# Tiles 2 and 3 turned by VectorE instead of TensorE, tiles 26 and 27 given their bias in the bank, and a new order, in a fused mean, linear and ReLU kernel

## The chip, the cores and the metric

The kernel runs on one core of one Trainium2 chip. The metric is the device time of one execution in microseconds (us), median of the runs. "us" also stands for the times in the trace, which are counted from the first instruction of the program.

## The reference

`x` has the shape (4, 1024, 512), `cond` (4, 256), `W` (1536, 512) and `b` (512), all float32. What is computed:

```python
hidden = concatenate([cond_512, cond_512], axis=-1)
x_mean = mean(x, axis=1, keepdims=True)
fused = concatenate([x, x_mean * ones_L, hidden[:, None, :] * ones_L], axis=-1)
relation = relu(einsum('bld,do->blo', fused, W) + b)
return x + relation
```

So every row of `x` is multiplied by the first third of `W`; the mean of its batch row by the second third and the condition by the last third are the same for all 1024 rows of a batch row, and together with `b` they make one bias vector per batch row. ReLU, and `x` is added.

## The kernel before

The 4096 rows of `x` are 32 tiles of 128 rows; batch row r is tiles 8r to 8r+7. A tile's product is 128x512 by 512x512. The contraction has J = 4 blocks of 128. Since float32 is split into a high and a low part (float32r), each block takes three matmuls, high by high, low by high and high by low (`product`, L355, L365): 12 for each tile, 384 in all, each 512 columns wide except that tile 31 is done in two halves of 256 columns. All of them add up in one of five PSUM banks (`bank`, L352, tile number modulo 5).

TensorE wants `x` with the contraction on the partitions, so every tile must be turned. Tiles 0 to 3, units 0 to 3 of one tile each, are turned by TensorE (`BY_PE`, L76): `x` arrives in its natural layout (tasks `X0.0` to `X0.3`), is gathered by a copy (`y`, L231), and a matmul by the identity turns it (`T`, L262, four for each tile). The other 28 tiles are seven units of four tiles, numbered 4 to 10. For them `x` is loaded a second time, in four quarters of 32 partitions (`Z`, L176, rows of 512 B), into one of three z buffers, and VectorE turns a block of all four tiles at once (`T`, L264, 32 by 32 blocks). After that ScalarE copies the turned block into the high part and takes its row sums for the mean in the same instruction (`h`, L270), and VectorE or GpSimd subtracts for the low part (`l`, L276). The high and low parts of `W` are made likewise (`wh`, L213, `wl`, L221).

The bias of a batch row is summed up on VectorE from the loaded parts of `W` (`c`, L302, `m`, L318), folded and spread over the partitions by one matmul by ones (`pb`, L342), and copied out by ScalarE (`bc`, L346).

A finished bank leaves in one of three ways (`WAYS`, L19). K (tiles 0 to 11): copied out (`K`, L428), bias added by GpSimd (`b`, L435), ReLU on ScalarE (`r`, L443), `x` added by GpSimd or VectorE (`F`, L450). B (tiles 12 to 27): `K`, L439, adds the bias on the way out, then `r` and `F` as before. I (tiles 28 to 31): ScalarE writes the bias into the bank before its first product (`P`, L418, L398), and one VectorE instruction does ReLU and the sum (`F`, L422, L402). Then SyncE stores the tile (`S`).

The order in which each engine does all this is the list `ORDER` (L22): a name is a task, `@d`, `@a` and `@p` put it on VectorE, ScalarE or GpSimd, and `fill` is a matmul on zeros. Nothing else schedules the work. `p2.0.1` is tile 2, block 0, second of the three matmuls; `p3.0` is all three; `31.0l` is a half. All loads but one and all stores are issued by SyncE in the order of the list, and share one queue.

```python
UNITS = [(t, 1) for t in range(4)] + [(t, 4) for t in range(4, NT, 4)]
BY_PE = (0, 1, 2, 3)
X_PARTS = {0: [(i, 1) for i in range(4)]}
```

## Time and profile before

| what | us |
|---|---|
| median of 3 runs | 101.08 |
| the three runs | 100.9, 101.08, 105.57 |
| the profiled execution | 101.22 |
| its span in the trace | 99.5 |
| outside of the span | 1.72 |

The profile is of one execution. The span runs from the first instruction of the program to the last one; the execution has 1.72 us around it. PE is TensorE's matmul queue, PEld its loads of the stationary operand, DVE is VectorE, ACT ScalarE, POOL GpSimd, SP SyncE, which only issues transfers here. A matmul's duration in the trace overlaps the next one's: what it costs is the distance from start to start.

### The profile page before, as it was taken

The page shows a single profiled execution, that of the slowest core. Times are in us where ns is not written, and L with a number is a line of the kernel's source. Part 1 is how long each engine was busy: PE and PEld are TensorE (multiplying, and loading weights), DVE is VectorE, ACT ScalarE, POOL GpSimd, SP SyncE. Part 2 cuts the span into 40 slices and gives each one's busy share as a digit, 9 for nine tenths or more (in the row PEclk, how much of TensorE's full clock was granted, in tenths as well). Part 3 has the DMA queues.
Part 4 walks back from the last instruction along what each step waited for, and adds up shares of the span by engine and source line. Part 5 has one row for each costly group of instructions (what it writes and reads, how often), then busy time and mean ns, then how long its engine had stood idle before and what let it go on. Part 6 is the DMA issues. An engine that isn't in the chain of part 4 may idle for free.

```text
span 99.5 us, 1446 instructions
## 1 busy us (share of the span) xinstructions
PE 95.0 (96%) x425; PEld 76.2 (77%) x425; DVE 80.2 (81%) x144; ACT 58.2 (58%) x153; POOL 65.1 (65%) x65
## 2 busy tenths in 40 slices
...
GB/s 43 376 375 239 210 199 212 278 394 314 222 209 212 215 254 269 209 223 275 259 212 242 328 294 268 308 133 264 390 315 366 208 275 285 404 406 406 398 385 123
DMA packets 25361, 27.36 MB, mean 275 GB/s; under 512 B 1413, under 2 KB 16009, under 8 KB 25354
## 3 DMA queue, kind: packets, MB, share of 16 engines
q1 hardware_dynamic: 25210, 27.01, 100.8%
q10 hardware_dynamic: 144, 0.26, 0.7%
q8 instruction: 3, 0.05, 0.2%
...
## 4 chain that ended last, share of the span: by engine, by line
PE 93%; ACT 2%; DVE 1%; issue 0%
PE po L365 87%; PE po L132 4%; ACT hi L271 1%; PE acc L343 1%; DVE x L403 1%; ACT o L235 1%; PE po L262 0%; DVE lo L277 0%; PE acc L262 0%; PE px L262 0%; DVE warm L123 0%; DVE one L124 0%
## 5 line engine op out<-in xcount | busy, mean ns | idle before, releaser
L365 PE MATMUL po<-w_hi,lo 128*128 128x512 f32 (+1 forms) x132 | 50.6, 386 | 0.1
L365 PE MATMUL po<-w_lo,hi 128*128 128x512 f32 (+1 forms) x132 | 50.5, 385 | 0.0
L365 PE MATMUL po<-w_hi,hi 128*128 128x512 f32 (+1 forms) x132 | 50.4, 386 | 0.0
L277 POOL TENSOR_TENSOR lo<-xT,hi 128x512 fp32r<-128x512 f32 x14 | 18.6, 1335 | 23.5 <-ACT hi L271 23.5
L365 PEld LDWEIGHTS po<-w_hi,lo 128*128 128x128 f32 x132 | 24.9, 188 | 5.7 <-DVE lo L277 0.7
L365 PEld LDWEIGHTS po<-w_hi,hi 128*128 128x128 f32 x132 | 24.7, 188 | 5.3 <-issue 0.4
L365 PEld LDWEIGHTS po<-w_lo,hi 128*128 128x128 f32 x132 | 24.8, 188 | 4.7
L454 POOL TENSOR_TENSOR x<-o,x 128x512 f32<-128x512 f32 x19 | 26.3, 1406 | 1.5 <-ACT o L447 1.5
L447 ACT ACTIVATE o<-o 128x512 f32<-128x512 f32 x28 | 16.2, 620 | 1.6 <-DVE o L440 1.3
L436 POOL TENSOR_TENSOR o<-o,bias 128x512 f32<-128x512 f32 x12 | 15.5, 1309 | 1.4 <-ACT bias L347 1.4
L271 ACT ACTIVATE hi<-px 128x512 fp32r<-128x512 f32 (+1 forms) x20 | 9.9, 495 | 4.9 <-DVE px L264 2.6
L319 DVE SCALAR_TENSOR_TENSOR acc<-w_mean,tot,acc 128x512 f32<-128x512 f32 x16 | 12.0, 750 | 0.6
L440 DVE TENSOR_TENSOR o<-po,bias 128x512 f32<-128x512 f32 x16 | 10.7, 677 | 1.7 <-PE po L365 1.7
L277 DVE TENSOR_TENSOR lo<-px,hi 128x512 fp32r<-128x512 f32 (+1 forms) x20 | 10.9, 558 | 1.1 <-ACT hi L271 1.0
L271 ACT ACTIVATE hi<-xT 128x512 fp32r<-128x512 f32 x14 | 8.8, 627 | 3.0 <-DVE xT L264 3.0
L264 DVE STREAM_TRANSPOSE px<-z 128x512 f32<-128x512 f32 x14 | 9.9, 707 | 0.0
L264 DVE STREAM_TRANSPOSE xT<-z 128x512 f32<-128x512 f32 x14 | 9.6, 690 | 0.2
L432 ACT ACTIVATE o<-po 128x512 f32<-128x512 f32 x10 | 5.6, 599 | 5.6 <-PE po L365 5.6
L454 DVE TENSOR_TENSOR x<-o,x 128x512 f32<-128x512 f32 x9 | 8.0, 914 | 0.9 <-ACT o L447 0.9
L303 DVE SCALAR_TENSOR_TENSOR acc<-wc,cT,acc 128x512 f32<-128x512 f32 x8 | 6.0, 746 | 0.3
L132 PE MATMUL po<-warm 128*128 128x512 bf16 x9 | 4.1, 614 | 1.0 <-DVE one L124 1.0
L327 ACT ACTIVATE fold<-acc 64x512 f32<-64x512 f32 x4 | 2.4, 597 | 4.4 <-DVE acc L319 4.4
...
## 6 DMA issues: line engine op xcount, KB each, us to landing
out_dram<-x SPq DMA_DIRECT2D x31, 256.0 KB, 4.0
z<-in_x_dram SPq DMA_DIRECT2D x28, 256.0 KB, 8.0
...
x<-in_x_dram SPq DMA_DIRECT2D x4, 256.0 KB, 3.9
...
w_mean<-in_L_cond_W_dram SPq DMA_DIRECT2D x4, 256.0 KB, 7.4
x<-in_L_cond_W_dram SPq DMA_DIRECT2D x3, 256.0 KB, 4.1
x<-in_L_cond_W_dram ACTq DMA_DIRECT2D x1, 256.0 KB
```

The lines of the kernel that those rows point to most:

```text
L132: nc.tensor.matmul(ps_o[2], lhsT=warm, rhs=warm.rearrange("p (o d) -> p o d", o=1).to_broadcast([P, 4, P]), start=True, stop=True,)
L264: nc.vector.transpose(xT.rearrange("p (n q e) -> p n q e", q=Q // E, e=E), zs[z_of(u)][:, : n * NQ].rearrange("p n (q j e) -> p n j q e", ...
L271: nc.scalar.activation(his[buf][:, col : col + m], xT, AF.Copy, accum_out=sums[:, r, j, s : s + 1])
L277: nc_of[e].tensor_tensor(los[buf][:, col : col + m], xT, his[buf][:, col : col + m].bitcast(F32), ALU.subtract)
L303: nc.vector.scalar_tensor_tensor(acc, wc[:, k], cT[:, k, r : r + 1], acc, ALU.mult, ALU.add)
L319: nc.vector.scalar_tensor_tensor(acc, w_mean[:, j, :], tot[:, r, j : j + 1], acc, ALU.mult, ALU.add)
L365: nc.tensor.matmul(v, lhsT=a[:, col : col + P], rhs=m, start=WAYS[t] != "I" and key not in done, stop=done.count(key) == 3 * J - 1, skip_g ...
L432: nc.scalar.activation(o, bank(t), AF.Copy)
L436: nc_of[e].tensor_tensor(o, o, biases[r], ALU.add)
L440: nc.vector.tensor_tensor(o, bank(t), biases[r], ALU.add)
L447: nc.scalar.activation(o, o, AF.Relu)
L454: nc_of[e].tensor_tensor(x_tile(t), o, x_tile(t), ALU.add)
```

## The change

- Tiles 2 and 3 become unit 2 of two tiles, `UNITS` and `BY_PE` say so. Their natural loads `X0.2` and `X0.3` leave the head of the program and become one load, `X0.2`, in its middle. Four half-size quarters `Z2.0` to `Z2.3` (8 of the 16 columns of z, 128 KB each) are issued behind the blocks of `W`. Two gathers and eight TensorE turns go; four VectorE turns of 128x256 come, and the eight `h` and eight `l` of 128x128 become four and four of 128x256. The old units 4 to 10 are now 3 to 9.
- Tiles 26 and 27 go way I instead of way B.
- `ORDER` is a new list throughout. Work changes engines in it: `wl0` and `wl1` go to GpSimd, `wh0`, `wh1` and `wh3` to ScalarE, and at the end GpSimd adds `x` to tiles 18 and 25 and no longer to tile 24.

```diff
-WAYS = "KKKKKKKKKKKKBBBBBBBBBBBBBBBBIIII"
+WAYS = "KKKKKKKKKKKKBBBBBBBBBBBBBBIIIIII"
...
-W0@a X0.0 fill X0.1 relu fill X0.2 fill W1 fill W2 fill fill W3 fill y0.2@d y0.0@d X0.3 y0.1@d fill Z4.0 wh0r@d T0.0
+W0@a X0.0 fill X0.1 relu fill W1 fill W2 fill fill W3 fill Z2.2 y0.1@p fill y0.2@d Z2.1 y0.0@d T0.1 T0.2 wh0l@a Z2.0
...
+p1.2.1 T2.0 p1.1.2 T2.1 Z4.1 p1.3.2 h2.0 p1.0.0 T2.3 p0.3.1 l2.0@d p0.3.2 h2.3 K1@d p2.0 h2.1 Z4.3 l2.3@d p3.0
+l2.1@p l0.1@d T2.2 p3.3 h2.2 Z4.2 l2.2@d p2.3 p0.2.1 p0.1.1 C p2.2 K0@d B p3.1 V T3.2 M2 p2.1 T3.1 h3.2 p3.2 M3 h3.1
+l3.2@d p4.2 K2@a T3.3 l3.1@p T3.0 p7.2 M1 h3.3 p5.1 h3.0 l3.3@p l3.0@d p6.1 M0 p4.0 to0 T4.1 Z5.2 p5.0 Z5.0 T4.0
...
-    UNITS = [(t, 1) for t in range(4)] + [(t, 4) for t in range(4, NT, 4)]
-    BY_PE = (0, 1, 2, 3)
-    Y_PARTS = {0: [(0, 1), (1, 1), (2, 2)], 1: [(0, 2), (2, 2)], 2: [(0, 2), (2, 2)]}
+    UNITS = [(0, 1), (1, 1), (2, 2)] + [(t, 4) for t in range(4, NT, 4)]
+    BY_PE = (0, 1)
+    Y_PARTS = {0: [(0, 1), (1, 1), (2, 2)], 1: [(0, 2), (2, 2)]}
     X_SLOT = [2, 3, 4, 5, 0, 1, 2, 3]
-    X_PARTS = {0: [(i, 1) for i in range(4)]}
+    X_PARTS = {0: [(0, 1), (1, 1), (2, 2)]}
...
-    sums = sb("sums", [P, B, J, 5])
+    sums = sb("sums", [P, B, J, 4])
...
-    pre = sb("pre", [P, J, 3])
+    pre = sb("pre", [P, J, 2])
...
-        2: [(pa, 1), (pb, 1), (pa, 2), (pb, 2)], 3: [(acc, 2), (acc, 3), (o4, 2), (o4, 3)],
...
-                xT = (turned if j % 2 else ps_x)[j // 2]
+                xT = (turned if j % 2 else ps_x)[j // 2][:, :m]
```

`to0`, which adds up the row sums of batch row 0, has two additions instead of three, since there are four units in it and not five.

What SyncE issues first, before: `x_65` takes tiles 0 to 3, `x_63` the blocks of `W` (block 0 goes out on ScalarE's queue), `z_69` and `z_70` the quarters of tiles 4 to 7 and 8 to 11.

```order
L146 DMA x_65<-in_x_dram 128x512 x3
L146 DMA x_63<-in_L_cond_W_dram 128x1x512 x3
L146 DMA x_65<-in_x_dram 128x512
L146 DMA z_69<-in_x_dram 32x16x128 x4
L146 DMA z_70<-in_x_dram 32x16x128 x4
L146 DMA bias_121<-in_cond_dram 4x256
```

And after, where `z_69` is first used for the half-size quarters of tiles 2 and 3, and `z_70` and `z_71` take tiles 4 to 7 and 8 to 11:

```order
L145 DMA x_65<-in_x_dram 128x512 x2
L145 DMA x_63<-in_L_cond_W_dram 128x1x512 x3
L145 DMA z_69<-in_x_dram 32x8x128 x4
L145 DMA z_70<-in_x_dram 32x16x128 x4
L145 DMA z_71<-in_x_dram 32x16x128 x4
L145 DMA bias_121<-in_cond_dram 4x256
```

Each block of `W` stands one place further to the front, and what followed the last block is now four short transfers with 512 B rows where one of 2 KB rows stood.

What VectorE does around its first turn, before: `lo_91` to `lo_93` are the low parts of tiles 1 to 3, `px_141` and `xT_123` the turned blocks of the first unit of four tiles.

```order
L277 TENSOR_TENSOR lo_91<-po_139,hi_76 128x128
L277 TENSOR_TENSOR lo_92<-px_141,hi_77 128x128
L277 TENSOR_TENSOR lo_93<-acc,hi_78 128x128 x2
L277 TENSOR_TENSOR lo_93<-po_140,hi_78 128x128 x2
L264 STREAM_TRANSPOSE px_141<-z_69 128x512
L264 STREAM_TRANSPOSE xT_123<-z_69 128x512
L277 TENSOR_TENSOR lo_94<-px_141,hi_79 128x512
```

And after, where the 128x256 rows are tiles 2 and 3, `o_106<-po_137` and `o_105<-po_136` are the tasks K1 and K0, and `px_142<-z_70` is T3.2, the first turn of tiles 4 to 7:

```order
L262 STREAM_TRANSPOSE px_141<-z_69 128x256
L262 STREAM_TRANSPOSE xT_123<-z_69 128x256
L262 STREAM_TRANSPOSE xT_124<-z_69 128x256
L275 TENSOR_TENSOR lo_92<-px_141,hi_77 128x256
L426 COPY o_106<-po_137 128x512
L275 TENSOR_TENSOR lo_93<-xT_124,hi_78 128x256
L275 TENSOR_TENSOR lo_90<-px_142,hi_75 128x128
L262 STREAM_TRANSPOSE px_142<-z_69 128x256
L275 TENSOR_TENSOR lo_93<-px_142,hi_78 128x256
L426 COPY o_105<-po_136 128x512
L262 STREAM_TRANSPOSE px_142<-z_70 128x512
L262 STREAM_TRANSPOSE xT_123<-z_70 128x512
```

Three turns now stand before the first low part of tile 2, and the copies K1 and K0 before the first turn of tiles 4 to 7.

What ScalarE does around the last bias, before: `bias_121` is batch row 3's, `po_139` the bank of tile 28.

```order
L447 ACTIVATE o_115<-o_115 128x512
L447 ACTIVATE o_116<-o_116 128x512
L347 ACTIVATE bias_121<-acc 128x512
L419 ACTIVATE po_139<-bias_121 128x512
L419 ACTIVATE po_136<-bias_121 128x512
```

And after, where `po_137` is the bank of tile 26 and `po_138` of tile 28:

```order
L443 ACTIVATE o_111<-o_111 128x512
L343 ACTIVATE bias_121<-acc 128x512
L415 ACTIVATE po_137<-bias_121 128x512
L443 ACTIVATE o_113<-o_113 128x512
L443 ACTIVATE o_112<-o_112 128x512
L443 ACTIVATE o_115<-o_115 128x512
L415 ACTIVATE po_139<-bias_121 128x512
L415 ACTIVATE po_140<-bias_121 128x512
```

The bias of tile 26 is now written right behind the copy of the bias itself, and TensorE's list has six matmuls (`p23.2`, `p24.3`) between `pb3` and the first product of tile 26.

## Rows read from the trace of the kernel before

**Rows 1.** The page: busy time of each engine, share of the span, instructions.

```profile
PE 95.0 (96%) x425; PEld 76.2 (77%) x425; DVE 80.2 (81%) x144; ACT 58.2 (58%) x153; POOL 65.1 (65%) x65
```

**Rows 2.** Chain that ended last, in order of time: start, us, engine, tile, line.

```profile
0.97 3.60 PE po L132 x8
...
63.00 19.04 PE po L365 x84
...
95.72 0.78 DVE x L403 x2
```

**Rows 3.** Timeline of TensorE, head: start, us, instruction; L365 products, L262 turns.

```profile
5.24 0.50 PE L365 MATMUL po<-w_hi,hi 128*128 128x512 f32 x1
...
14.04 0.39 PE L365 MATMUL po<-w_lo,hi 128*128 128x512 f32 x1
14.27 0.38 PE L262 MATMUL acc<-ident,o 128*128 128x128 f32 x2
14.41 0.48 PE L365 MATMUL po<-w_lo,hi 128*128 128x512 f32 x1
14.72 0.39 PE L365 MATMUL po<-w_hi,lo 128*128 128x512 f32 x1
```

**Rows 4.** SyncE's timeline: when the last block of W and Z4.2 were issued.

```profile
3.42 0.60 SPq L146 DMA_DIRECT2D x<-in_L_cond_W_dram  x1
...
6.39 0.49 SPq L146 DMA_DIRECT2D z<-in_x_dram  x1
```

**Rows 5.** The same two transfers: count, KB each, us from issue to landing.

```profile
x<-in_L_cond_W_dram SPq DMA_DIRECT2D x1, 256.0 KB, 4.2
...
z<-in_x_dram SPq DMA_DIRECT2D x1, 256.0 KB, 8.1
```

**Rows 6.** Stretches: busy of PE, PEld, DVE, ACT, POOL; clock, DMA share, GB/s.

```profile
4.00:6.00 2.00, 2.00 (x11) 1.38 (x9) 1.84 (x8) 1.07 (x6) 0.00 (x0) 1.00 0.98 366
10.00:12.00 2.00, 2.00 (x11) 1.65 (x10) 1.96 (x6) 0.94 (x4) 0.00 (x0) 1.00 1.23 210
64.00:66.00 2.00, 2.00 (x10) 1.66 (x9) 1.82 (x4) 1.59 (x6) 2.00 (x3) 1.00 0.32 88
...
94.00:96.00 2.00, 2.00 (x17) 1.80 (x15) 0.97 (x2) 0.00 (x0) 0.00 (x0) 1.00 1.03 391
```

**Rows 7.** Groups of instructions by line and shape: count, busy us, mean ns, idle before.

```profile
L454 POOL TENSOR_TENSOR x<-o,x 128x512 f32<-128x512 f32 x19 | 26.3, 1406 | 1.5 <-ACT o L447 1.5
...
L440 DVE TENSOR_TENSOR o<-po,bias 128x512 f32<-128x512 f32 x16 | 10.7, 677 | 1.7 <-PE po L365 1.7
L264 DVE STREAM_TRANSPOSE px<-z 128x512 f32<-128x512 f32 x14 | 9.9, 707 | 0.0
...
L454 DVE TENSOR_TENSOR x<-o,x 128x512 f32<-128x512 f32 x9 | 8.0, 914 | 0.9 <-ACT o L447 0.9
...
L271 ACT ACTIVATION_READ_ACCUMULATOR hi<-px 128x1 f32 x20 | 3.9, 195 | 0.0
...
L235 ACT ACTIVATE o<-x 128x256 f32<-128x256 f32 x2 | 0.8, 411 | 0.0
```

**Rows 8.** Timeline of VectorE, first unit of four: first turn to first low part.

```profile
16.48 0.71 DVE L264 STREAM_TRANSPOSE px<-z 128x512 f32<-128x512 f32 x1
...
17.95 0.69 DVE L277 TENSOR_TENSOR lo<-px,hi 128x512 fp32r<-128x512 f32 x1 [0.18 <-ACT hi L271]
```

**Rows 9.** Timeline around the last bias: the matmul pb3, bc3 and P28.

```profile
81.88 0.39 PE L343 MATMUL acc<-v_acc,ones 128*128 128x512 f32 x1
...
82.30 0.60 ACT L347 ACTIVATE bias<-acc 128x512 f32<-128x512 f32 x1 [0.38 <-PE acc L343]
...
82.93 0.60 ACT L419 ACTIVATE po<-bias 128x512 f32<-128x512 f32 x1
```

**Rows 10.** Timeline of the end: GpSimd's last additions of x, SyncE's last stores.

```profile
90.16 3.07 POOL L454 TENSOR_TENSOR x<-o,x 128x512 f32<-128x512 f32 x2 [1.54 <-ACT o L447]
...
96.17 0.83 SPq L146 DMA_DIRECT2D out_dram<-x  x2
```

More of the change, by code (lines that the diff above doesn't have):

```diff
@@ L42 @@
-r17@a p22.0 T9.3 F7@p X6.0 K18 p21.1 h9.3 X3.0 S5 c3.0 F8@p p22.3 r10@a S4 T10.2 p21.0 S2 S7 K20 l9.3@p p21.3 h10.2
-X5.0 l9.0@d r18@a p23.2 T10.1 F6@p p23.0 T10.3 p25.1 K21 b9@p h10.3 p22.2 T10.0 h10.1 p23.3 c3.1 h10.0 X6.1 p26.0
-X7.0 r15@a F18@d r9@a p25.3 to3 K19 F10@p r14@a p22.1 m3.0 r19@a p26.3 m3.1 F9@p p26.2 m3.2 p24.1 m3.3 F17@p S9
-p25.2 S6 K22 f3 S18 p24.0 F12@p S8 fa3 p25.0 vh3 F19@d p23.1 r20@a X7.1 F13@p p24.3 r22@a S10 K23 S17 p27.1 vl3
-r23@a l10.3@p p26.1 l10.0@d r11@a pb3 F23@d p27.2 bc3@a F11@p l10.2@d S23 P28 p27.0 S19 K25 p24.2 S12 F15@p K26 P30
@@ new lines @@
+p0.0.1 h1.1 p0.0.2 wh2@d Z3.2 h1.0 T1.3 p1.1.0 h0.3 l1.0@d p1.0.2 h1.2 wl2@d p0.2.0 h1.3 p1.2.0 wh3@a wl1@p Z3.1
+l1.1@d p1.2.2 l1.3@d p1.0.1 l1.2@d h0.1 p1.1.1 l0.2@d p0.2.2 p1.3.0 wl3@d p0.1.2 Z4.0 p0.3.0 l0.3@d p0.1.0 p1.3.1
+p1.2.1 T2.0 p1.1.2 T2.1 Z4.1 p1.3.2 h2.0 p1.0.0 T2.3 p0.3.1 l2.0@d p0.3.2 h2.3 K1@d p2.0 h2.1 Z4.3 l2.3@d p3.0
+l2.1@p l0.1@d T2.2 p3.3 h2.2 Z4.2 l2.2@d p2.3 p0.2.1 p0.1.1 C p2.2 K0@d B p3.1 V T3.2 M2 p2.1 T3.1 h3.2 p3.2 M3 h3.1
+l3.2@d p4.2 K2@a T3.3 l3.1@p T3.0 p7.2 M1 h3.3 p5.1 h3.0 l3.3@p l3.0@d p6.1 M0 p4.0 to0 T4.1 Z5.2 p5.0 Z5.0 T4.0
@@ new lines @@
+p7.0 h4.1 Z5.1 t3 as0 p7.1 t0 T4.2 h4.0 p7.3 T4.3 K3@a p4.1 l4.0@d h4.3 p6.3 K7@a ac0@d Z5.3 h4.2 p8.0 ac1@p t2 t1
+p6.2 c0.0 p4.3 Z6.0 l4.1@p c0.1 p5.3 K4@a m0.0 p5.2 Z6.1 l4.3@p m0.1 p8.1 K5@a m0.2 p6.0 Z6.3 m0.3 p9.1 l4.2@d Z6.2
+f0 p10.1 K6@a fa0 p8.3 Z7.2 vh0 p9.0 vl0 p10.2 T5.1 Z7.3 p11.3 T5.2 h5.1 p10.0 T5.3 Z7.1 l5.1@p pb0 p11.1 T5.0 bc0@a
+as1 p9.3 b2@p Z7.0 h5.2 c1.0 p8.2 h5.0 p9.2 c1.1 b0@p X4.1 h5.3 p11.0 X0.2 l5.2@d K8@a p10.3 l5.0@d to1 r0@a X1.0
+b3@p T6.0 K9@a X1.1 p13.1 K10@a T6.1 p12.2 h6.0 l5.3@p m1.0 p12.0 r3@a m1.1 h6.1 p15.0 b1@p m1.2 p15.2 m1.3 p13.3
@@ new lines @@
+F0@p r1@a p14.3 T6.2 f1 T6.3 p15.1 l6.1@p h6.2 fa1 Z9.0 p13.0 Z8.0 l6.0@d vh1 b5@p p12.1 Z8.1 h6.3 T7.0 Z9.2 p15.3
+vl1 l6.3@p p11.2 l6.2@d p13.2 T7.2 K11@a r2@a pb1 T7.1 p12.3 Z8.3 bc1@a F2@p p16.1 as2 K13 h7.2 p16.3 Z8.2 T7.3 F3@p
+h7.1 p14.2 K15 h7.3 p18.1 c2.0 Z9.1 b7@p h7.0 p18.2 c2.1 p18.0 Z9.3 l7.2@d to2 r7@a l7.1@p p16.0 K12 m2.0 p14.1 F1@p
+p14.0 m2.1 p17.1 m2.2 b4@p S1 p16.2 X2.1 m2.3 S3 p17.2 K14 b6@p X3.0 f2 p18.3 X4.0 r5@a fa2 p17.0 l7.3@p l7.0@d vh2
+p19.3 r4@a T8.2 p20.2 b10@p vl2 h8.2 p19.0 T8.1 F5@p l8.2@d p19.1 T9.2 pb2 p20.0 bc2@a T8.3 F4@p as3 p20.3 K18 r12@a
@@ new lines @@
+p17.3 K16 F7@p S4 h8.1 S0 p19.2 T8.0 r6@a X5.0 K17 p20.1 l8.1@p X2.0 h8.3 S7 p21.2 h8.0 K20 S5 l8.3@p r15@a p21.1
+l8.0@d X6.0 h9.2 S2 p22.0 T9.1 X3.1 F6@p T9.0 p25.2 h9.1 T9.3 p25.1 h9.0 b8@p S6 K19 h9.3 p25.3 X5.1 c3.0 p22.1 to3
+r8@a c3.1 b11@p p23.3 X7.0 m3.0 p21.0 b9@p m3.1 r11@a p21.3 r18@a m3.2 p25.0 X6.1 F11@p r9@a p24.1 m3.3 r10@a p24.2
+f3 F8@p p23.0 r13@a fa3 p22.2 vh3 F10@p p22.3 r19@a vl3 p24.0 K21 F9@p S10 S8 p23.1 F19@d pb3 S9 p23.2 bc3@a l9.1@p
+S11 l9.2@d P26 p24.3 K23 r21@a p26.3 r20@a F21@d p26.1 r23@a F12@p K24 S21 p26.2 P28 K22 P29 p26.0 l9.3@p S12 P27
```

36 lines of the change are left out of this document (9 added, 27 removed).

## The prediction

> **What bounds the kernel now.** I read the busy times first: TensorE is busy for 95.0 of 99.5 us, VectorE for 80, the others for less [rows 1]. Then the chain of waits in order of time: it runs on TensorE almost without a break until 95.72, then through two VectorE instructions of tile 31, then the last stores [rows 2]. 84 products take 19.04 us there, 0.2267 us each; this step is the unit of what follows. The 384 products, 372 of 512 columns and 24 halves, can't be had for less, so there are only three places where a change can gain or lose: the head, before products come at that pace; matmuls between the products; the end, behind the last one.
>
> The head is measured by one number: the start of the n-th product less (n-1) steps of 0.2267, the time by which the products run late. In the list 32 products stand before the one that starts at 14.72 [rows 3], so before it is 14.72 - 32 x 0.2267 = 7.47 us. The first product starts at 5.24 [rows 3]; of the 2.23 us between, the turns are the larger part: from 14.04 to 14.72 there are two products, 0.45 us, and two turns, so a turn costs 0.115 us, and the twelve behind the first product 1.4. The other 0.8 us are waits for copies, high and low parts.
>
> **The change part by part.** *Eight turns go.* 8 x 0.115 = 0.92 us less on TensorE, all on the path.
>
> *But TensorE has less to do early.* Only 22 of the 24 products of tiles 0 and 1 stand before `p2.0`, the first of the new unit. From 5.24 they take 22 x 0.2267 = 5.0 us, four turns 0.5 and waits as before 0.8: done at 11.5. Moving `wl0`, `wl1` and one gather to GpSimd and `wh` to ScalarE is inside this: dearer there or not, it costs nothing while tile 2 is ready later than 11.5.
>
> *When do the quarters land?* The last block of `W` was issued at 3.42 and landed 4.2 us later, at 7.6; `Z4.2`, behind `X0.3` and three quarters, was issued at 6.39 and landed at 14.5 [rows 4, 5]. Between the two lie 6.9 us. A 256 KB block of wide rows takes 0.7 us at 366 GB/s, a quarter of 512 B rows 1.25 us at 210 GB/s [rows 6]: 0.7 + 4 x 1.25 = 5.7, and 1.2 us are left as lag of the landing behind the data. After the change `X0.2` no longer stands before `W`, so the last block lands 0.7 earlier, at 6.9; the four half quarters take 4 x 0.625 = 2.5, to 9.4. The trace shows no half quarter, so the lag is bounded: none (9.4), or twice that of the four whole ones (11.8). I take the 1.2 us, for the same number of transfers in the same queue: **10.6**. The Skill speaks against the row here: the Trainium skill, DMA: Bandwidth & Descriptors, Specifications, lets transfers run at line rate from 512 B on. By that the four would take 1.4 us and land at 9.5; 210 GB/s against 366 contradicts it [rows 6].
>
> *From there to the products.* `T2.0` waits for all four quarters, 10.65. A turn of 512 columns takes 0.71 [rows 7]; one of 256 I put at 0.41, as a 256-column copy on ScalarE [rows 7], between half of 0.71 and all of it. `h2.0` then takes 0.41 and the reading of its sums 0.195, half of it overlapped: 11.6. VectorE has `T2.1` and `T2.3` before `l2.0` and starts that at 11.75, done at 12.15. `p2.0.1`, the 24th product, goes at 12.2 and is late by 12.2 - 23 x 0.2267 = 7.0. The wait of about half a microsecond in front of it is new.
>
> *Behind it, what is late next.* VectorE's queue has K1, `l2.3`, `T2.2`, `l2.2` and K0 before `T3.2`. K0 waits for `p0.1.1`, the 36th product: start 12.2 + 12 x 0.2267 = 14.9, end 0.39 later, and K0 takes 0.68, as the other reads of a bank [rows 7]. So `T3.2` starts at 16.0; its quarters, 4 x 1.25 behind, land at 15.6 and don't decide. From the first turn of a unit of four to the end of its first low part went 17.95 + 0.69 - 16.48 = 2.16 us [rows 8], with the same two turns before it as now. `p4.2.1`, the 50th product, goes at 18.2: late by 18.2 - 49 x 0.2267 = 7.1. `T3.0` and `l3.0` after it come out for `p4.0.1` at 20.9, no later than that. So the head comes down from 7.47 to 7.1: **0.37 us gained**, of the 0.92 of the turns; the rest goes into the wait for the quarters.
>
> *The second load of tiles 2 and 3* moves 0.5 MB more, 2.5 us of the queue at the rate of quarters. It pushes later loads; what hides it is the hole at 64 to 66, where the queue ran at 88 GB/s, 32% busy [rows 6]. Without that cover it reappears as stores at the end, 0.5 MB at 391 GB/s = 1.3 us.
>
> *Tiles 26 and 27.* Each loses a bank read with bias (0.68), a ReLU and an addition (0.91 on VectorE [rows 7]) and gains a write of the bias, 0.60 on ScalarE [rows 9], and one VectorE instruction, taken as the bank read's 0.68. VectorE gains 2 x 0.91 us near the end, beside TensorE: nothing on the path. The wait that it adds: `p26.3` stands six products behind `pb3`, 0.23 + 6 x 0.2267 = 1.59 us, and now needs the copy of the bias, then `P26`. From `pb3` to the end of the first such write were 82.93 + 0.60 - 81.88 = 1.65 us [rows 9], and 0.05 for the signal: **0.1 lost**. Behind `P26` on ScalarE stand ReLUs and `P28`, which has over 2 us.
>
> *The end.* F31 and the last two stores [rows 2, 10] are what they were: 0.
>
> The sum is made against the profiled execution, 101.22 with its span of 99.5: 101.22 - 0.37 + 0.1 = 100.95. The median of the runs shown is 0.14 below it: **100.8 us**.
>
> **The rivals.** *The quarters land later (slower).* Every 0.1 us after 10.6 is 0.1 us, since `l2.0`, K0 and `T3.2` shift with it. The gain is gone at a landing of 10.9; at the bound of 11.8 it is 1.2 - 0.27 = 0.9 us slower than before, 102.0. For it: the queue is already full (share 1.23) when whole quarters go through [rows 6], and those of tiles 4 to 7 are queued right behind. Against it: a block of wide rows landed within 4.2 us although issued into a full queue [rows 5].
>
> *The quarters land early.* With no lag, or at the rate of wide rows (0.7 us for 256 KB, so 1.4 for all four), they land by 9.5, `p2.0.1` goes right behind the 22 products at 11.75, K0 ends by 15.5, `p4.2.1` goes at 17.7: late by 6.6, 0.9 us gained, 100.3; with the 0.8 us of waits gone too, 100.0 at the least. For it: 9.4 is plain bytes by rate. Against: the landing of `Z4.2`, which plain bytes put at 13.3.
>
> *The end moves to GpSimd.* It was busy throughout its middle and now adds `x` once more in all (1.41 us [rows 7]), tile 25's as its last, and the stores of 25, 30 and 31 stand behind one another on SyncE. Before, its last two additions took 1.5 us each after a wait of 1.54 and ended at 93.2 [rows 10]; one more brings 94.7 if that wait stays. The last issue was in the 0.83 us from 96.17; at 0.42 for each store the one of tile 25 may go as late as 95.3 without harm. So it is covered by 0.6 us; if GpSimd slips by 2 us through waits for ScalarE, or the 0.5 MB isn't absorbed, the time is some 101.2 + 0.3 to 1.0: 101.9.
>
> *The clock falls.* The eight fills ran 0.45 us apart [rows 2], 512 columns near the lower level of 1.2 GHz, the products at 0.2267, near 2.4; the granted clock is 1.00 in every stretch that I read [rows 6]. The Trainium skill, TensorE: Matmul & The Clock Gate, What's actually happening, has the slower level as the state after idleness. If the waits around 11.5 brought it back for some ten products, that is 10 x 0.22 = 2.2 us: 103.0. Before, TensorE had waits of that size only among the turns, with no such effect.
>
> **How the numbers follow.** The forecast, quarters at about 10.6 and little else: 0.60. Quarters late enough to lose: 0.19. Early: 0.11. End at GpSimd or the stores: 0.08. Clock: 0.02. The likeliest case has its own range of 100.4 to 101.1. To hold 8 in 10 the range takes in most of the early case and of the late one: 100.2 to 101.8. A measurement of this kernel tells about 2% from no change, 2.02 us. Faster than that would be below 99.06: even the head without any wait gives only 100.0, so 0.01. Slower, above 103.1, needs the clock or two slower cases together: 0.04. Within: 0.95.
>
> **What would show it.** Right: eight turns instead of sixteen, a first 512-column product near 5.2, VectorE idle before its first 128x256 turn until 10.5 to 10.8 with a transfer of z as releaser, TensorE waiting about 0.5 us before the 23rd or 24th product, the 50th at about 18.2, products in steps of 0.227 after that, SyncE's last issue 0.3 us earlier. Wrong: the turn starting before 10 or after 11.2; waits of TensorE after 20 us (for banks, `P26`, low parts from GpSimd); a product step of 0.43; SyncE's last stores held by GpSimd instead of TensorE.

## The result and the profile after

The changed kernel took 102.79 us (median of 22 runs, 101.59 to 103.72), the kernel before 102.75 in 22 runs between them; the ratio is 1.0103 with a 95% interval of 1.0068 to 1.0138. So the change made the kernel 1.0% slower, about 1.0 us, where 0.3 us less was forecast. That is within the 2% that the prediction called no change, but 102.79, and also 1.0103 times the 101.08 shown ahead (102.1), lie above its range of 100.2 to 101.8. Some executions of either kernel (7 of 22 and 12 of 22) are in a slower state and take some per cent longer, so the ratio here (medians 102.2 and 101.3 us) and those below compare the others alone, two of six with e7_before_load and five or more with each other run.

The profiled execution took 102.06 us with a span of 100.3 us, against 101.22 and 99.5 before. Busy times of the page of the changed kernel, to be read beside [rows 1]:

```profile
PE 94.7 (94%) x417; PEld 75.3 (75%) x417; DVE 79.2 (79%) x133; ACT 57.9 (58%) x146; POOL 68.6 (68%) x69
```

TensorE has eight instructions and 0.3 us less, as the turns went; the span is longer all the same. The chain that ended last in the changed kernel, in order of time (start, us, what), beside [rows 2]:

```profile
1.63 4.54 DMA x<-in_L_cond_W_dram
...
7.36 0.29 DVE lo L275
7.66 1.28 DVE w_lo L221
...
8.98 26.85 PE po L361 x116
...
78.22 18.17 PE po L361 x90
...
96.42 0.42 DVE x L399
```

Before, the chain ran over TensorE from its fills on, with short pieces of ScalarE and VectorE between. Now TensorE's part begins at 8.98: up to there it waits for a low part of `W` on VectorE. Behind the last product stands one addition of tile 31, where the chain before had two, and then the stores. The same place in the timeline of the changed kernel, VectorE, GpSimd and TensorE:

```profile
6.81 0.43 DVE L217 CAST w_hi<-x 128x512 fp32r<-128x512 f32 x1 [0.94 <-DMA x<-in_L_cond_W_dram]
...
6.89 1.48 POOL L221 TENSOR_TENSOR w_lo<-x,w_hi 128x512 fp32r<-128x512 f32 x1 [0.63 <-ACT w_hi L215]
...
7.57 1.36 DVE L221 TENSOR_TENSOR w_lo<-x,w_hi 128x512 fp32r<-128x512 f32 x1
...
8.98 0.50 PE L361 MATMUL po<-w_lo,hi 128*128 128x512 f32 x1 [0.58 <-DVE w_lo L221]
```

`wl2` on VectorE takes 1.36 us beside `wl1` on GpSimd; the next one on VectorE, `wl3`, takes 0.68 in the same program:

```profile
9.64 0.68 DVE L221 TENSOR_TENSOR w_lo<-x,w_hi 128x512 fp32r<-128x512 f32 x1
...
10.45 0.46 DVE L262 STREAM_TRANSPOSE px<-z 128x256 f32<-128x256 f32 x1
10.82 0.73 DVE L262 STREAM_TRANSPOSE xT<-z 128x256 f32<-128x256 f32 x2
```

The last two rows are the first turns of tile 2. No idle time stands before them: VectorE was busy until 10.45, and the quarters (issued from 3.59, 5.0 us to landing in the middle) were there at 10.4. TensorE ran 22 products up to 12.5 and went on with tile 2 without a stop.

Around tile 26, ScalarE and TensorE in the timeline of the changed kernel, which answer to [rows 9]:

```profile
77.83 0.39 PE L339 MATMUL acc<-v_acc,ones 128*128 128x512 f32 x1
...
78.26 0.60 ACT L343 ACTIVATE bias<-acc 128x512 f32<-128x512 f32 x1 [1.36 <-PE acc L339]
...
78.89 0.60 ACT L415 ACTIVATE po<-bias 128x512 f32<-128x512 f32 x1
...
79.19 0.39 PE L361 MATMUL po<-w_lo,hi 128*128 128x512 f32 x1
...
79.55 0.19 PEld L361 LDWEIGHTS po<-w_hi,hi 128*128 128x128 f32 x1 [0.39 <-ACT po L415]
79.55 0.50 PE L361 MATMUL po<-w_hi,hi 128*128 128x512 f32 x1
...
79.88 0.39 PE L361 MATMUL po<-w_hi,lo 128*128 128x512 f32 x1
```

From 79.19 to 79.88 there are two steps, 0.69 us instead of 0.45: TensorE loses 0.13 us to the wait for `P26` and another 0.11 in the step behind it.

Where the 0.8 us of the two spans went, then: the 50th product starts at 18.70 (before 18.69), so the head gave nothing in this profile; tile 26 cost 0.24, and the last product starts 0.34 later, at 96.10; the rest, 0.5 us, lies behind it, in the stores. Stretches at the end of the changed kernel (busy time of PE, PEld, DVE, ACT, POOL; clock, DMA share, GB/s):

```profile
80.00:84.00 4.00, 4.00 (x19) 3.27 (x18) 3.92 (x6) 3.33 (x8) 2.77 (x2) 1.00 0.85 322
84.00:88.00 4.00, 4.00 (x20) 3.36 (x19) 1.81 (x4) 3.51 (x7) 3.54 (x3) 1.00 0.88 287
88.00:92.00 4.00, 4.00 (x20) 3.36 (x19) 3.55 (x5) 0.39 (x1) 4.00 (x4) 1.00 1.02 390
92.00:96.00 4.00, 4.00 (x27) 3.62 (x26) 1.50 (x3) 0.00 (x0) 2.19 (x2) 1.00 1.05 403
96.00:100.00 4.00, 0.38 (x4) 0.17 (x2) 0.42 (x1) 0.00 (x0) 0.00 (x0) 1.00 0.71 260
```

And of the kernel before:

```profile
80.00:84.00 4.00, 4.00 (x19) 3.30 (x19) 3.90 (x7) 2.86 (x6) 4.00 (x4) 1.00 0.89 250
84.00:88.00 4.00, 4.00 (x20) 3.30 (x19) 3.15 (x6) 3.10 (x6) 4.00 (x3) 1.00 1.05 405
88.00:92.00 4.00, 4.00 (x21) 3.36 (x20) 4.00 (x6) 1.98 (x4) 2.46 (x3) 1.00 1.06 406
92.00:96.00 4.00, 4.00 (x28) 3.58 (x26) 2.24 (x5) 0.00 (x0) 1.23 (x1) 1.00 1.04 395
```

This is the view that the prediction should have been made from. The queue is full at 405 GB/s. At 80 us both kernels have 6.5 to 6.7 MB left to move (changed: 4 x (322 + 287 + 390 + 403 + 260) GB/s x us = 6.65 MB), and 6.6 MB at 405 GB/s take 16.3 us: the data can't be out before 96.3 us, which is about when TensorE ends. So the end is tied to the stores as much as to TensorE, and a hole in the queue after 80 us can show in the time. From 80 to 96 us the changed kernel loses 16 x 405 - 4 x (322 + 287 + 390 + 403) = 870 KB, 2.2 us of a full queue; the kernel before 660 KB, 1.6 us. The changed kernel has two holes there, in stretches of 2 us:

```profile
82.00:84.00 2.00, 2.00 (x10) 1.64 (x9) 2.00 (x5) 1.75 (x4) 0.77 (x1) 1.00 0.64 238
...
86.00:88.00 2.00, 2.00 (x11) 1.69 (x11) 0.00 (x0) 1.51 (x3) 2.00 (x2) 1.00 0.73 200
```

They go with SyncE's waits (changed kernel, 79 to 98 us: what it waited for, us in total, times, the longest):

```profile
SPq L145 <- DVE x L450: 3.0, 3, 2.2
SPq L145 <- POOL x L450: 1.5, 3, 0.8
```

SyncE issues in the order of the list. At 79.3 us it comes to `S21`, whose addition on VectorE ends at 81.61, and for 2.2 us issues nothing, though the load `X7.1`, five places behind, could go: in the run that moves it ahead of `S21` it goes out at 78.79. The first hole follows. Between 86 and 90 us it stands at single stores of GpSimd's additions in the same way, and from 88 us on the rest goes through a full queue.

### The profile page after: what moved, and what is told of

The parts are those of the page before. It is cut to its first block, busy times and chain, and to the rows that moved or that the text cites. A ratio compares the mean times of both kernels' runs of the same rounds, so it can differ in the third digit from the quotient of the medians.

```text
span 100.3 us, 1413 instructions
## 1 busy us (share of the span) xinstructions
PE 94.7 (94%) x417; PEld 75.3 (75%) x417; DVE 79.2 (79%) x133; ACT 57.9 (58%) x146; POOL 68.6 (68%) x69
## 3 DMA queue, kind: packets, MB, share of 16 engines
q1 hardware_dynamic: 26282, 27.54, 99.8%
HBM read 19.40 MB, written 8.39 MB: 277 GB/s over the span
## 4 chain that ended last, share of the span: by engine, by line
PE 87%; DMA 5%; DVE 2%; ACT 1%; SPq 1%; issue 0%
PE po L361 86%; DMA x<-in_L_cond_W_dram 5%; DVE w_lo L221 1%; PE acc L339 1%; SPq L145 1%; ACT w_hi L215 1%; ACT hi L269 1%; DVE x L399 0%; DVE lo L275 0%
## 5 line engine op out<-in xcount | busy, mean ns | idle before, releaser
L275 POOL TENSOR_TENSOR lo<-xT,hi 128x512 fp32r<-128x512 f32 (+1 forms) x15 | 20.2, 1352 | 18.4 <-ACT hi L269 18.4
L443 ACT ACTIVATE o<-o 128x512 f32<-128x512 f32 x26 | 15.4, 623 | 2.6 <-POOL o L432 2.5
L269 ACT ACTIVATE hi<-px 128x512 fp32r<-128x512 f32 (+2 forms) x18 | 9.6, 532 | 6.5 <-DVE px L262 6.2
L275 DVE TENSOR_TENSOR lo<-px,hi 128x512 fp32r<-128x512 f32 (+2 forms) x18 | 10.8, 603 | 1.5 <-ACT hi L269 1.5
L269 ACT ACTIVATE hi<-xT 128x512 fp32r<-128x512 f32 (+1 forms) x16 | 9.6, 601 | 3.7 <-DVE xT L262 3.7
L262 DVE STREAM_TRANSPOSE px<-z 128x512 f32<-128x512 f32 (+1 forms) x16 | 10.8, 673 | 0.2
L262 DVE STREAM_TRANSPOSE xT<-z 128x512 f32<-128x512 f32 (+1 forms) x16 | 10.3, 647 | 0.1
L436 DVE TENSOR_TENSOR o<-po,bias 128x512 f32<-128x512 f32 x14 | 9.1, 669 | 0.0
L419 DVE SCALAR_TENSOR_TENSOR x<-po,x 128x512 f32<-128x512 f32 x5 | 3.4, 682 | 4.5 <-PE po L361 4.5
L450 DVE TENSOR_TENSOR x<-o,x 128x512 f32<-128x512 f32 x6 | 5.9, 1001 | 0.2 <-ACT o L443 0.2
```

The costliest lines, as they stand in the source:

```text
L262: nc.vector.transpose(xT.rearrange("p (n q e) -> p n q e", q=Q // E, e=E), zs[z_of(u)][:, : n * NQ].rearrange("p n (q j e) -> p n j q e", ...
L269: nc.scalar.activation(his[buf][:, col : col + m], xT, AF.Copy, accum_out=sums[:, r, j, s : s + 1])
L275: nc_of[e].tensor_tensor(los[buf][:, col : col + m], xT, his[buf][:, col : col + m].bitcast(F32), ALU.subtract)
L419: nc.vector.scalar_tensor_tensor(x_tile(t), bank(t), 0.0, x_tile(t), ALU.max, ALU.add)
L436: nc.vector.tensor_tensor(o, bank(t), biases[r], ALU.add)
L443: nc.scalar.activation(o, o, AF.Relu)
```

## The experiments

Each run was compared in five rounds with the kernel before. The table has, worked out from one profile of each kernel, the start of the 8th, 50th and last product (the 396th, since tile 31 has 24 halves; the expectations speak of the 400th), what the queue lost from 80 to 96 us (16 us at 405 GB/s less the four stretches of 4 us, divided by 405), the MB that are left to move at 88 us, the span, and the ratio to the kernel before with its interval.

| run | 8th | 50th | last | lost | left | span | ratio (95%) |
|---|---|---|---|---|---|---|---|
| before | - | 18.69 | 95.76 | 1.6 | 3.9 | 99.5 | 1 |
| changed | 8.98 | 18.70 | 96.10 | 2.2 | 4.2 | 100.3 | 1.0103 (1.0068 to 1.0138) |
| e1_wl1_vector | 8.48 | 18.22 | 95.58 | 2.1 | 4.0 | 100.8 | 1.0030 (0.9976 to 1.0084) |
| e2_pb3_early | 9.36 | 19.11 | 96.33 | 1.8 | 4.3 | 101.3 | 1.0060 (1.0002 to 1.0119) |
| e3_adds_vector | 8.70 | 18.44 | 95.84 | 2.5 | 4.2 | 100.5 | 1.0078 (1.0023 to 1.0133) |
| e4_all | 8.70 | 18.45 | 95.69 | 2.4 | 4.0 | 101.0 | 1.0080 (1.0012 to 1.0149) |
| e5_load_early | 8.45 | 18.18 | 95.57 | 1.4 | 3.5 | 99.2 | 0.9971 (0.9939 to 1.0002) |
| e6_head_queue | 8.74 | 18.48 | 95.72 | 1.1 | 3.6 | 99.8 | 0.9957 (0.9923 to 0.9990) |
| e7_before_load | - | 18.46 | 95.53 | 2.8 | 4.4 | 101.1 | 1.0155 (1.0096 to 1.0214) |
| e8_bias_out | 8.76 | 18.49 | 95.61 | 3.7 | 4.4 | 101.8 | 1.0215 (1.0173 to 1.0256) |
| e9_one_load | 8.77 | 18.49 | 95.83 | 2.3 | 4.2 | 100.4 | 1.0070 (1.0027 to 1.0113) |
| e10_head_vector | 8.37 | 18.10 | 95.31 | 1.2 | 3.4 | 99.2 | 0.9963 (0.9924 to 1.0002) |
| e11_bias_out_apart | 8.37 | 18.11 | 95.18 | 3.1 | 4.2 | 100.7 | 1.0146 (1.0072 to 1.0219) |

Read the columns against one another: the start of the last product moves by 1.2 us over these runs and doesn't order the ratios (the earliest, 95.18, has the third worst ratio). Four runs have it within 0.1 us, at 95.5 to 95.6 (e1, e5, e7 and e8), and ratios from 0.9971 to 1.0215. The queue does order them, roughly: the four slowest lost 2.2 to 3.7 us and have 4.2 to 4.4 MB left at 88 us, the three below 1 lost 1.1 to 1.4 and have 3.4 to 3.6 left. The loss is a rough measure, since it also counts stretches in which the DMA engines were busy throughout and moved less than 405 (share 1.03 at 382 GB/s, 92 to 96 us of e11).

The 8th product has to be read with care. Before it the cast of `W2` waits for a block of `W` to land, and that landing differs from profile to profile: in the seven with the changed kernel's head (the changed one, e2, e3, e5, e8, e9 and e11) the cast starts at 6.20 to 7.01 us, the 8th product 2.2 to 2.4 us behind it, at 8.37 to 9.36.

**The low part of W back on VectorE.**

```diff
-p1.2.0 wh3@a wl1@p Z3.1 l1.1@d p1.2.2
+p1.2.0 wh3@a Z3.1 l1.1@d wl1@d p1.2.2
```

> Edit: the low part of W's second quarter goes from GpSimd back to VectorE, behind the low part of tile 1's second block; nothing else moves. Theory A (the subtraction on GpSimd slows the one on VectorE beside it): VectorE's low part of W2 takes 0.7 us instead of 1.36, the eighth product starts at 8.2 to 8.4 us instead of 8.98, the 24th (first of tile 2 that is late) near 12.0, and the 400th 0.4 to 0.7 us earlier than in the changed kernel; the time is 0.4 to 0.7 us below it, at or below the kernel before. Rival B (the W blocks land late in this traffic and set the eighth product, whoever subtracts): the low part of W2 still takes over 1.1 us or starts later, the eighth product stays within 0.2 us of 8.98, the time within 0.2 us of the changed kernel. Rival C (tile 2's turns, held by VectorE and the quarters, are late anyway): the eighth product is early, but the idle time comes back at the 24th or 50th product, and the 50th still starts within 0.15 us of the changed kernel's.

`wl2` of this run, in VectorE's timeline:

```profile
6.27 0.43 DVE L217 CAST w_hi<-x 128x512 fp32r<-128x512 f32 x1 [0.33 <-DMA x<-in_L_cond_W_dram]
...
7.75 0.68 DVE L221 TENSOR_TENSOR w_lo<-x,w_hi 128x512 fp32r<-128x512 f32 x1
```

0.68 instead of 1.36: theory A holds for the mechanism. What it was worth in time isn't shown. The 8th product starts at 8.48 and the 50th at 18.22, 0.5 us earlier than in the changed kernel's profile, with no wait at tile 2 (so rival C falls); but in e5_load_early, whose head is the changed kernel's, they start at 8.45 and 18.18, and the cast of `W2` starts there when it does here:

```profile
6.27 0.43 DVE L217 CAST w_hi<-x 128x512 fp32r<-128x512 f32 x1 [0.34 <-DMA x<-in_L_cond_W_dram]
```

So the half microsecond goes with the landing, which is rival B's cause. In the run with all three edits the cast started at 7.42 and the 8th product only 1.3 us behind it; what the edit gains depends on the landing. The ratio came down by 0.7%, with intervals that overlap.

**The bias row one block, three products, earlier.**

```diff
-S8 p23.1 F19@d pb3 S9
+S8 pb3 p23.1 F19@d S9
```

> Edit: the product that spreads the third bias row stands one product earlier on TensorE; nothing else moves. Theory A (TensorE's stop at tile 26's last product delays all behind it): the bias copy and ScalarE's write of the bias into tile 26's bank end 0.2 us earlier or more, the stop of 0.13 + 0.11 us goes, the 400th product starts 0.2 us earlier and the time is 0.2 us lower than the changed kernel's. Rival B (the queue of stores sets the end, not TensorE): the stop goes, the 400th product starts 0.2 us earlier, and the last store's issue and the time stay where they are, within 0.1 us.

The stop at `p26.3` went, but half of it, 0.12 us, came back in the step behind the moved `pb3` (0.34 us), whose operand was now ready only 0.06 us before it. The run's own head was worse by chance, and shows the hold that GpSimd has on VectorE more sharply than the edit made for it. GpSimd's `wl1`, and VectorE's cast of `W2` beside it:

```profile
6.95 1.28 POOL L221 TENSOR_TENSOR w_lo<-x,w_hi 128x512 fp32r<-128x512 f32 x1 [0.77 <-ACT w_hi L215]
...
7.01 1.50 DVE L217 CAST w_hi<-x 128x512 fp32r<-128x512 f32 x1 [1.04 <-DMA x<-in_L_cond_W_dram]
```

The cast began 0.06 us after GpSimd's subtraction, and what takes 0.43 elsewhere took 1.50. What TensorE's 0.24 us are worth in time this run can't say.

**Three additions to VectorE.**

```diff
-l9.0@d p29.2 r22@a F15@p
+l9.0@d p29.2 r22@a F15@d
...
-p27.3 F13@p
+p27.3 F13@d
...
-P31r F14@p
+P31r F14@d
```

> Edit: three of the late additions (tiles 15, 13, 14) go from GpSimd to VectorE, at their places in the order. Theory A (GpSimd's last additions, back to back to 94.2 us, hold SyncE's stores in a queue that has no gap up to the last issue): GpSimd's last addition ends about 90.5 us, SyncE has a gap before its last issue, the last issue ends 0.3 to 0.6 us earlier at the same 400th product, and the time is 0.3 to 0.5 us below the changed kernel's. Rival B (the stores' own traffic sets the tail, whatever the additions do): GpSimd ends early, the last issue keeps its distance of 0.7 us to the last addition, the time moves less than 0.15 us. Rival C (VectorE takes over as the late one: three additions of 0.9 us): the last additions on VectorE or TensorE's late products move later and the time rises by up to 0.5 us.

GpSimd ended its last addition at 90.68 instead of 94.19, and nothing was gained: theory A falls as stated. SyncE's waits from 79 us on in this run:

```profile
SPq L145 <- DVE x L450: 3.3, 4, 2.2
SPq L145 <- DVE x L419: 2.5, 2, 1.9
```

The 1.9 us are `S29`: its addition stands behind `F14` on VectorE now, and `S18`, `S17` and `S25`, whose additions had ended at 87.3, 89.0 and 90.7, stood behind it in SyncE's list when it went out at 91.9. It isn't how early the additions are that counts, but whether the next one in SyncE's list is. This is rival C's price in another form.

**The three together.** The edits are those of the three runs above.

> Edit: the three edits of the low part of W's second quarter (to VectorE), the bias row (one product earlier) and the three late additions (to VectorE) together. Theory A (three separate losses on one chain): the gains add, 0.6 + 0.2 + 0.4 = 1.2 us below the changed kernel, some 0.2 us below the kernel before. Rival B (the queue of stores alone sets the end): not more than the run with the three additions gains. Rival C (tile 2 is late anyway): not more than 0.6 us below the changed kernel, so not below the kernel before.

Nothing added up: the last product is 0.4 us earlier than in the changed kernel, the queue loses 2.4 us, the ratio is that of the third edit alone. Rival B.

**One load earlier.** The theory that these four left standing is the queue with SyncE's order:

```diff
-S11 l9.2@d P26
+S11 X7.1 l9.2@d P26
...
-p27.2 r24@a X7.1 l9.0@d
+p27.2 r24@a l9.0@d
```

> Edit: the load of tiles 30 and 31 (0.5 MB) goes six places to the front of SyncE's list, ahead of the store of tile 21, where SyncE waits 2.3 us in the changed kernel with the transfers running at 230 to 255 GB/s; nothing else moves. Theory A (the changed kernel's end is set by the bytes that are left when the queue is full again at 88 us, since SyncE is held at single stores before): 0.5 MB less is left after 88 us (3.7 instead of 4.2 MB), SyncE's last issues wait for their additions again (idle time of 0.2 us or more before the last four), the last store lands 0.4 to 0.9 us sooner after TensorE's last product than in the changed kernel, and the time is 0.4 to 0.9 us lower. Rival B (TensorE's last product sets the end, the stores follow it at a fixed distance): no change within 0.2 us. Rival C (the load in the full stretch before 80 us delays other transfers that TensorE or VectorE wait for): waits of VectorE's or GpSimd's additions for x appear, the time rises.

Stretches of this run, to be read beside those of the changed kernel:

```profile
80.00:84.00 4.00, 4.00 (x19) 3.27 (x19) 4.00 (x6) 3.33 (x8) 2.30 (x3) 1.00 1.01 362
84.00:88.00 4.00, 4.00 (x21) 3.35 (x20) 1.37 (x4) 2.99 (x6) 4.00 (x4) 1.00 0.97 371
88.00:92.00 4.00, 4.00 (x21) 3.35 (x20) 3.85 (x5) 0.39 (x1) 4.00 (x3) 1.00 0.97 364
92.00:96.00 4.00, 3.85 (x26) 3.38 (x24) 1.23 (x3) 0.00 (x0) 1.66 (x2) 1.00 1.01 384
```

287 has become 371 GB/s, 3.5 MB were left after 88 us instead of 4.2, and the last two stores wait for their additions again (the last four were expected to). Moving one load took 1.3% off, more than any other single edit, with intervals apart (0.9939 to 1.0002 against 1.0068 to 1.0138): theory A. Of the 1.1 us between the two spans 0.5 us are the head, which the edit doesn't touch and which was early here by chance; the other 0.6 us lie behind the last product, within the 0.4 to 0.9 expected. The ratio goes over twelve executions, and the two other runs with this load early have 0.9957 and 0.9963.

**Head and queue together.** The edits of the first, second and fifth run, and `S19` behind `X7.1` too, ahead of `S21`.

> Edit: the low part of W's second quarter on VectorE, the bias row one product earlier, and in SyncE's list the load of tiles 30 and 31 and the store of tile 19 ahead of the store of tile 21; the additions stay as in the changed kernel. Theory A (three losses on one chain, the queue of stores being the one that hid the gain of the other two in the runs so far): the 400th product starts at 95.3 to 95.7 us, the last store lands within 2.2 us of the last addition, and the time is 1.0 to 1.5 us below the changed kernel, 0.2 to 0.5 us below the kernel before. Rival B (the stores' own traffic, 0.5 MB more, sets the end): the time stays at that of the run with the low part of W moved alone.

0.9957 (0.9923 to 0.9990): some 0.4 us below the kernel before and 1.5% below the changed one, the only run whose whole interval lies below 1. Against the run with the load alone the ratio is 0.14% lower, less than either interval, so what the head adds here isn't shown.

**The kernel before with the second load.**

```diff
-T7.0 p14.0 X1.0 b4@p
+T7.0 p14.0 XX X1.0 b4@p
...
+    @task("XX")
+    def _(e):
+        dma(e, out=xs[X_SLOT[2]][:, :2], in_=xv[0, :, 2:4, :])
```

> Edit: the kernel before, with one more load of 0.5 MB (tiles 2 and 3 once more, into a slot that is free) ahead of the load of tiles 4 and 5, where the changed kernel has its second load of tiles 2 and 3; nothing reads it. Theory A (the second load is absorbed in the hole of the queue at 64 to 66 us, as the prediction says): the time rises by less than 0.2 us, bytes left after 88 us as before (3.9 MB). Rival B (it isn't absorbed, the queue is full from there to the end but for holes that SyncE's waits make): 0.2 to 0.5 MB more is left after 88 us and the time rises by 0.4 to 1.3 us.

The time is rival B's, 1.5% and a little above its range, from two executions alone. TensorE's last product is 0.2 us earlier than in the kernel before; all of the loss is in the queue. Three of its stretches:

```profile
64.00:66.00 2.00, 2.00 (x10) 1.66 (x9) 1.82 (x4) 1.59 (x5) 2.00 (x2) 1.00 0.55 212
...
80.00:84.00 4.00, 4.00 (x19) 3.30 (x19) 3.94 (x7) 2.86 (x6) 4.00 (x4) 1.00 0.51 149
84.00:88.00 4.00, 4.00 (x20) 3.30 (x19) 3.15 (x6) 3.01 (x7) 4.00 (x3) 1.00 1.04 378
```

And SyncE's longest wait from 79 us on, for a store (in the kernel before the same wait took 0.7):

```profile
SPq L146 <- DMA out_dram<-x: 2.2, 1, 2.2
```

The bytes themselves were absorbed, as theory A has it: the hole at 64 to 66 us moved 212 GB/s instead of 88, and at 80 us both kernels have 6.5 MB left. But SyncE holds at `X7.1` for the landing of a store that frees its slot, and issues it at 82.10 instead of 80.47. While it holds, the additions' stores pile up behind, 4.4 MB instead of 3.9 are left at 88 us, and 17 stores then go out without a gap until 97.8. That the extra load made that store land later is argued from the order of the queue.

**Tiles 26 and 27 the old way.**

```diff
-S11 l9.2@d P26 p24.3
+S11 l9.2@d p24.3
...
-p28.2 F26 p29.1
+p28.2 K26 r26@a F26@d p29.1
...
-p28.1 F27 p29.0
+p28.1 K27 r27@a F27@d p29.0
...
-        o = parks[park_of[t]]
+        o = wc[:, t - 26] if t >= 26 else parks[park_of[t]]
```

> Edit: tiles 26 and 27 of the changed kernel get their bias on the way out again, as in the kernel before (bank read with bias and addition on VectorE, ReLU on ScalarE, parked in memory that is dead by then); no bias is written into their banks. Theory A (the bias in the bank costs TensorE the stop of 0.24 us at tile 26's last product and gains nothing at the end, VectorE having idle time there): the stop is gone, the 400th product starts 0.2 us earlier, the time moves by 0.0 to 0.2 us down. Rival B (VectorE's saved 1.8 us are what lets the last additions and their stores go in time): the additions of tiles 22 and 27 to 29 end 0.5 us later or more, the stores behind them too, and the time rises by 0.3 to 0.8 us.

Rival B, by more than it asked: TensorE's stop is gone and its last product 0.5 us earlier, but the time is 1.1% above the changed kernel. So in this order the bias in the bank was worth something at the end, which the prediction had put at nothing. VectorE in this run:

```profile
87.96 0.69 DVE L436 TENSOR_TENSOR wc<-po,bias 128x512 f32<-128x512 f32 x1 [0.23 <-PE po L361]
89.35 1.40 DVE L450 TENSOR_TENSOR x<-wc,x 128x512 f32<-128x512 f32 x1 [0.70 <-ACT wc L443]
90.67 1.78 DVE L450 TENSOR_TENSOR x<-o,x 128x512 f32<-128x512 f32 x1
```

Two things make it late: the wait of 0.70 for the ReLU, which is of this edit's own order, and additions of 1.4 to 1.8 us. The last run takes the first away.

**The same with the wait taken out.**

```diff
-p28.2 K26 r26@a F26@d p29.1 F23@d S26 P31l r16@a p27.1 F20@d S23 r17@a
+p28.2 K26 r26@a p29.1 F23@d P31l r16@a p27.1 F20@d S23 F26@d S26 r17@a
...
-p28.1 K27 r27@a F27@d p29.0 F22@d S27 P31r F14@p p28.0 S22 F29
+p28.1 K27 r27@a p29.0 F22@d P31r F14@p p28.0 S22 F27@d S27 F29
```

> Edit: as the run with tiles 26 and 27 given their bias on the way out, but VectorE's addition of tile 26 stands two additions further back and that of tile 27 one, so that VectorE doesn't wait for ScalarE's ReLU between reading the bank and adding; their stores are moved with them. Theory A (what that run lost came from VectorE's two waits of 0.7 us for the ReLU): the waits are gone, the additions of tiles 22, 23 and 27 to 29 end within 0.5 us of the changed kernel's, and the time is within 0.3 us of the changed kernel's. Rival B (the two bank reads and the longer additions themselves, beside GpSimd's, are the price of the old way): the last additions and stores are still 0.5 us late or more and the time stays 0.5 to 1.2 us above the changed kernel's.

```profile
88.14 1.53 DVE L450 TENSOR_TENSOR x<-o,x 128x512 f32<-128x512 f32 x1
89.59 1.78 DVE L450 TENSOR_TENSOR x<-wc,x 128x512 f32<-128x512 f32 x1
91.29 0.68 DVE L419 SCALAR_TENSOR_TENSOR x<-po,x 128x512 f32<-128x512 f32 x1
```

The waits are gone, and `F29`, the last row, still starts 1.3 us later than in the changed kernel (90.00). Between the rivals, nearer to B: 0.4% above the changed kernel, with overlapping intervals, though its last product is 0.9 us earlier (0.6 us of that at the 8th already). An addition from memory stands beside GpSimd's additions for 1.5 to 1.8 us; one from a bank, as way I has it, takes 0.68 in the same stretch.

**The changed kernel without the second load.** The additions of tiles 2 and 3 add the parked result to itself, so the residual is left out there.

```diff
-p9.2 c1.1 b0@p X4.1 h5.3 p11.0 X0.2 l5.2@d
+p9.2 c1.1 b0@p X4.1 h5.3 p11.0 l5.2@d
...
-                nc_of[e].tensor_tensor(x_tile(t), o, x_tile(t), ALU.add)
+                nc_of[e].tensor_tensor(x_tile(t), o, o if t in (2, 3) else x_tile(t), ALU.add)
```

> Edit: the changed kernel without its second load of tiles 2 and 3 (0.5 MB); the additions of these two tiles add the parked result to itself instead of x, as long an instruction, so the residual is left out in two tiles; nothing else moves. Theory A (the second load is what fills the queue up to the end, as the kernel before with one more load showed): bytes left after 88 us fall from 4.2 to some 3.7 MB, SyncE's last issues wait for their additions again, the time is 0.8 to 1.4 us below the changed kernel, as with the load of tiles 30 and 31 moved. Rival B (the bytes are done with by 80 us whatever is loaded before, and only the place of the stores behind the one of tile 21 counts): 4.1 MB or more left after 88 us and the time within 0.3 us of the changed kernel.

```profile
80.00:84.00 4.00, 4.00 (x20) 3.28 (x19) 4.00 (x6) 3.43 (x8) 2.41 (x2) 1.00 0.79 295
84.00:88.00 4.00, 4.00 (x21) 3.35 (x20) 1.45 (x3) 3.15 (x7) 3.89 (x4) 1.00 1.04 297
```

Mostly rival B: the holes are there as before, 4.2 MB are left after 88 us, and the ratio is 0.3% lower, within the intervals. In the new order the second load is not what costs; the same 0.5 MB in the old order cost 1.5%. In these two pairs bytes ahead of a hole didn't count, only what they did to the wait that makes it.

**All early low parts of W on VectorE.** On top of the run with head and queue:

```diff
-T0.3 Z2.3 wl0l@p fill
+T0.3 Z2.3 fill
...
-y1.1@d y1.0@a wl0r@p l0.0@d
+y1.1@d wl0l@d y1.0@a l0.0@d wl0r@d
```

> Edit: the run with head and queue mended, with both halves of the low part of W's first quarter on VectorE too, so that GpSimd subtracts nothing before tile 2. Theory A (GpSimd's subtractions hold VectorE's beside them): the gather beside them takes 0.4 us instead of 0.70 to 0.78, the second product starts at 5.9 to 6.3 us instead of 6.3 to 6.75, the time is 0.1 to 0.5 us below that run. Rival B (VectorE, which now does 0.8 us more, and the landing of W's later blocks set tile 2): the 50th product stays at 18.2 to 18.5 us, the time within 0.15 us of that run.

```profile
4.86 0.29 DVE L236 COPY o<-x 128x256 f32<-128x256 f32 x1 [0.89 <-DMA x<-in_x_dram]
```

The gather takes 0.29, where it took 0.73 in the changed kernel, so theory A's mechanism holds again; but the second product still starts at 6.48, and the ratio, 0.9963, can't be told from that of the run without this edit. The time is rival B's; the 50th product, at 18.10, came a little before its range, but e11, where GpSimd does subtract, has 18.11.

## Why the prediction was wrong, step by step

The step that failed is *The end*, put at 0; two steps of the head failed as well, and what they cost isn't shown. In the order of the prediction:

*Eight turns go* and *TensorE has less to do early*: the turns went. The first product started at 5.59 instead of 5.24, and the 22 products ended at 12.5, not 11.5. The sentence that moving `wl0`, `wl1` and one gather to GpSimd "costs nothing while tile 2 is ready later than 11.5" failed as a mechanism: GpSimd's subtraction doubled the one beside it on VectorE, TensorE waited 0.8 us at its 8th product, and tile 2 was not what it then waited for. (`wh3` was on ScalarE before already.) In time it can't be told from the landing of `W`: the 50th product came at 18.11 to 19.11 in the seven profiles with this head and at 18.10 to 18.48 in the four with `wl1` on VectorE; 18.2 was predicted.

*When do the quarters land*: 10.6 predicted, 10.4 measured in the changed kernel's profile, and that is partly luck. The last block of `W`, issued at 2.94, was to land at 6.9, 0.7 us earlier for the load that went; it landed at 8.05, later than before:

```profile
x<-in_L_cond_W_dram SPq DMA_DIRECT2D x1, 256.0 KB, 5.1
```

The four half quarters then took 2.3 us and not 3.7, so two errors of opposite sign met. In the profiles of the experiments that keep this list of loads the block landed at 7.2 to 8.5 and the quarters at 9.4 to 10.7. It decided nothing: the low part of tile 2 was ready at 11.9, 0.9 us before its product, so an earlier landing would have gained nothing and a later one had room. In the run with `wl1` on VectorE 0.3 us of that room were left. The bound of 100.0 for a head without any wait doesn't come out of the prediction's terms: 7.47 less 5.24 and four turns of 0.115 is 1.8 us, which would make it 99.4; nothing hangs on it.

*What is late next*: the wait foreseen in front of the 24th product didn't come, since TensorE was late itself. From there the chain ran as predicted, shifted by half a microsecond: the 24th product at 12.73 (12.2), `T3.2` at 16.48 (16.0), the 50th at 18.70 (18.2). A 256-column turn took 0.46 and 0.40; 0.41 was taken.

*The second load*: in the old order the cover named, the hole at 64 to 66 us, did take the bytes, and the load cost 1.5% all the same, as far as the profile shows through SyncE's longer wait at `X7.1`. That this is near the 1.3 us which the prediction gave as the price without cover is luck. In the new order its removal moves 0.3%, within the uncertainty.

*Tiles 26 and 27*: the wait is 0.24 us and not 0.1, since a stop of TensorE costs the step behind it as well. "Nothing on the path" for VectorE's side was wrong in the other direction at least in one order: taken back, the bias in the bank costs 1.1% more there, and with ScalarE's wait taken out 0.4%, within the intervals.

*The end*, put at 0 because F31 and the last two stores are what they were, is the step that made the loss. The prediction read 391 GB/s at 94 to 96 us [rows 6] as a rate and not as a queue that is full from 84 us to the end. SyncE's new list loses 0.5 us more of that queue than the old one, its last issue ends 0.6 us later instead of 0.3 earlier, and moving one load in it takes 1.3% off, about all of the loss. The rival that came nearest is the end at GpSimd and the stores, 101.9 us with 0.08: the place was right, but the cause is SyncE's order, for GpSimd ended at 94.19, earlier than the 94.7 foreseen, and could be relieved by 3.5 us without gain.

The clock stayed at 1.00 in every stretch shown of the changed kernel; that rival did not occur.

What stays open: how the 1.0% divides between head, tile 26 and stores. In the two profiles they are 0.0, 0.24 and 0.5 us; in the runs, moving `wl1` alone gave 0.7% with intervals that overlap, which shows nothing, and moving the load 1.3%.
